# Graph attention on one core: score halves issued in the other order, and layer-norm normalizations moved from VectorE to ScalarE

## The chip, the cores and the metric

The kernel runs on one core of a Trainium2 chip. The metric is the time of one execution on the device, in microseconds (us); the median of several runs is compared. The profile comes from one further execution with the hardware profiler on.

The core's engines run side by side and each works through its own queue in program order: TensorE (PE in the rows, its weight loads PEld), VectorE (DVE), ScalarE (ACT), GpSimd (POOL), and SyncE (SP), which issues the DMAs. They wait for each other through semaphores. TensorE writes its results to PSUM, a small memory that VectorE and ScalarE read; GpSimd works on SBUF, the large on-chip memory, only.

## The reference

The input is `x` (8 frames, 2048 nodes, 256 channels, float32) and an adjacency matrix `adj` (2048 x 2048). With `LN(x) = (x - mean) * rsqrt(var + 1e-5)` over the channels:

```python
q, k, v = split(einsum('fnc,ck->fnk', x, w_qkv), 3)       # 8 heads of 32 channels
scores = einsum('fnhd,fmhd->fhnm', q, k) / sqrt(32)
attn   = softmax(where(adj > 0, scores, -1e9), axis=-1)
t      = einsum('fhnm,fmhd->fnhd', attn, v)
y      = LN(x + t) * ln1_g + ln1_b
h      = relu(y @ w1 + b1)
z      = LN(y + h @ w2 + b2) * ln2_g + ln2_b
out    = LN(x + z)
```

So each node passes three layer norms: after the attention, after the two-layer network, and after the outer residual.

## The kernel before

**The attention steps.** For each frame `f` the queries are cut in 4 chunks of 512 (`qc`), the 8 heads in 2 groups of 4 (`g`), the keys in 16 blocks of 128 (`mb`). One step handles one `(f, qc, g, mb)`; there are 8 x 4 x 2 x 16 = 1024 steps. In this text S(k) is the score part on TensorE of step k, A0(k) and A1(k) are its two additions on VectorE, E(k) its exponential on ScalarE, V(k) its value part on TensorE.

- `scores(item)` (L135 to L146). For each half (two heads) a PSUM tile `s` of 128 x 1024 takes the two heads' score matmuls, L142. Each head is a 32-row matmul in its own strip of 32 rows of the array and has two matmul instructions in the trace, so a step has 8. Then VectorE adds the mask out of PSUM into half of the tile `p` (L144: A0, then A1), and ScalarE takes the exponential of the whole tile `p` in place (L146: E).
- `values(item)` (L152 to L183). Four heads' value matmuls add into `o` (L161). In 9 of 16 blocks (`POOLED`, mb 0, 1, 3, 4, 6, 7, 9, 10, 12) GpSimd adds the tile `p` to `acc` (L165, L167: 8 additions to a group of 16 steps); in the others the row sums go through TensorE into `den` (L175). At the last block `acc` goes into `den` too, and ScalarE copies `o` and `den` out (L181, L183).
- The main loop emits S, A and E of step t+2, then V of step t, then one piece of filler work. The queues follow that order.
- `ps_s` has three PSUM tiles `s`, handed out in turn. Two of them go to each step, and one to every filler piece that needs PSUM. So between filler pieces the first half of step k reuses the tile that A1(k-2) freed, and the second half the tile that A0(k-1) freed. There are 5 tiles `p`; A(k) can be written once V and GpSimd are through with the tile of step k-5.

**The filler.** After 32 steps a chunk's `tail(f, qc)` (L204 to L275) is put in a queue and carried out a piece at a time, one piece per step, during the first half of the next chunk. It divides by the row sums, adds `x`, and does the three norms with the two-layer network between. A norm is `norm_stats` (L186: statistics on VectorE, L190 and L191, then `rs`, the inverse standard deviation, on GpSimd, L193 and L194), two pieces later `norm` (L197, L199: four VectorE instructions, one for each of 128 rows of the tile `y`), and then what follows:

- norm 1 (called at L232, filler piece of block 4): in the next piece TensorE transposes `y` (L237), ScalarE applies gain and bias (L240), GpSimd does the same on `y` itself (L242, L243); then L248 and L258 are the two-layer network and L260 its residual.
- norm 2 (L264, block 10): followed by three GpSimd operations on the same tile (L265 to L267).
- norm 3 (L274, block 15): followed by the store.

There are 32 tails, so 96 norms and 384 instructions at L199. In the last query chunk of a frame the projections of the next frame are filler too.

`general_path` runs only if a guard finds the row sums out of range.

Of the kernel before, what the change touches and what calls it, by code (L numbers as in the profile page):

```python
# [10 lines left out]
F32 = mybir.dt.float32  # L11
# [3 lines left out]
AF = mybir.ActivationFunctionType  # L15
ALU = mybir.AluOpType
AX = mybir.AxisListType

P = 128
H = 8  # L20
D = 32
CH = 512
# [30 lines left out]
def fast_path(ctx, tc, cst, x, adj, out, RS):  # L53
    nc = tc.nc
    F, N, C = x.shape
    NT, NCK, TPC, MB = N // P, N // CH, CH // P, N // P
# [10 lines left out]
    small = ctx.enter_context(tc.tile_pool(name="small", bufs=6))  # L67
    ps_s = ctx.enter_context(tc.tile_pool(name="ps_s", bufs=3, space=bass.MemoryType.PSUM))
# [32 lines left out]
    QT, KT, V = {}, {}, {}  # L101
# [33 lines left out]
    def scores(item):  # L135
        f, qc, g, mb = item
        pt = PT[item] = pp.tile([P, 4, CH], F32, name="p")
        for half in range(2):
            ps = ps_s.tile([P, 2, CH], F32, name="s")
            for j in range(2):  # L140
                r = D * (2 * half + j)
                nc.tensor.matmul(ps[:, j, :], KT[f, mb // TPC][r:r + D, g, (mb % TPC) * P:(mb % TPC + 1) * P],  # L142
                                 QT[f, qc][r:r + D, g, :], start=True, stop=True)
            nc.vector.tensor_tensor(pt[:, 2 * half:2 * half + 2, :], ps,  # L144
                                    mask[:, mb, qc * CH:(qc + 1) * CH][:, None, :].to_broadcast([P, 2, CH]), ALU.add)
        nc.scalar.activation(pt, pt, AF.Exp, scale=1.0 / math.sqrt(D))  # L146
# [48 lines left out]
        return mv, rs  # L195

    def norm(t, mv, rs):  # L197
        for j in range(TPC):
            nc.vector.tensor_scalar(t[:, j, :], t[:, j, :], mv[:, j, 0:1], rs[:, j:j + 1], op0=ALU.subtract, op1=ALU.mult)  # L199

    def rows(v):
        return v[:, None, :].to_broadcast([P, TPC, C])
# [1 line left out]
    def tail(f, qc):  # L204
# [25 lines left out]
        yield  # L230
        yield
        norm(y, mv, rs)  # L232
        yield
        py = ps_s.tile([P, 2, CH], F32, name="s")
# [27 lines left out]
        yield  # L262
        yield
        norm(z, mv, rs)  # L264
        nc.gpsimd.tensor_tensor(z, z, rows(cst["g2r"]), ALU.mult)  # L265
        nc.gpsimd.tensor_tensor(z, z, rows(cst["be2r"]), ALU.add)
# [5 lines left out]
        yield  # L272
        yield
        norm(z, mv, rs)  # L274
        nc.sync.dma_start(out[f, qc * CH:(qc + 1) * CH, :].rearrange("(j p) c -> p j c", p=P), z)  # L275

# [20 lines left out]
    for k in range(LEAD):  # L297
        scores(items[k])
    for t, item in enumerate(items):
        f, qc, g, mb = item  # L300
        if f == 0 and g == 0 and mb == 0 and qc + 1 < NCK:
            fill.append(mask_ahead(qc + 1))
        if f + 1 < F:
            if qc == NCK - 1 and g == 0 and mb == 0:
                fill.append(project(f + 1, 0))
                fill.append(project(f + 1, 1))
            if qc == NCK - 1 and g == 1 and mb == 9:
                fill.append(project(f + 1, 2))
                fill.append(project(f + 1, 3))
        if t + LEAD < len(items):  # L310
            nf, _, _, nmb = items[t + LEAD]
            while (nf, nmb // TPC) not in V:
                advance()
            scores(items[t + LEAD])
        values(item)
        if mb == MB - 1 and g == 1:
            fill.append(tail(f, qc))
        advance()
# [236 lines left out]
```

## Time and profile before

| what | value |
|---|---|
| median of 3 runs | 4457.56 us (4450.9 to 4458.03) |
| the profiled execution's own time | 4455.42 us |
| its span, first to last instruction | 4453.5 us |
| mean granted TensorE clock | 0.925 of full speed |
| busy: PE / DVE / ACT / POOL | 3876.9 / 3170.7 / 2259.6 / 2896.5 us |

How to read it: busy time is the union of an engine's instructions, as an average over stages with different limits. An instruction of VectorE or GpSimd that is held up after its start counts as busy for all that time. Windows of the trace are given in us from the start of the span. Where single stages are looked at, the chunk that starts at 908.8 us stands for the others.

### The profile page before, as it was taken

What the parts mean: (1) busy time and instruction counts of PE and PEld (TensorE: products, weight loads), DVE (VectorE), ACT (ScalarE), POOL (GpSimd) and SP (SyncE); (2) the same over time, 40 slices, a digit from 0 to 9 for tenths busy, and PEclk for the clock granted to TensorE, in tenths of its full rate; (3) what the DMA queues carried; (4) which work ended last, traced back from release to release, by engine and by line L of the source; (5) the groups of instructions that cost most, each with busy time, mean ns of one, the idle gap of its engine ahead of it and who ended that gap; (6) DMA issues with size and microseconds to landing.
All of it is one profiled execution on the core that took longest, in us unless ns stands there. A gap on an engine that the chain in (4) does not pass through costs nothing.

```text
span 4453.5 us, 56008 instructions
## 1 busy us (share of the span) xinstructions
PE 3876.9 (87%) x23556; PEld 1271.3 (29%) x23556; DVE 3170.7 (71%) x3463; ACT 2259.6 (51%) x1425; POOL 2896.5 (65%) x905
## 2 busy tenths in 40 slices
PE   7888898888988889888898888988889898888896
PEld 3222232222322223222232222322233222322222
DVE  2777757777478775778657876678856777577775
ACT  3644554555555545455455554455554455444553
POOL 1665647677467765678656776577765677567776
PEclk9988899999999999899999999999999899999998
DMA  3010000000000000000000000000000000000000
GB/s 108 10 48 29 20 29 10 10 10 1 29 10 10 10 29 1 10 10 10 29 1 10 10 10 29 1 10 10 10 29 1 10 11 10 29 10 6 6 10 15
DMA packets 62003, 72.72 MB, mean 16 GB/s; under 512 B 2993, under 2 KB 53297, under 8 KB 61745
## 3 DMA queue, kind: packets, MB, share of 16 engines
q1 hardware_dynamic: 61744, 69.09, 5.0%
q8 instruction: 186, 3.05, 0.3%
q14 instruction: 73, 0.59, 0.0%
HBM read 52.30 MB, written 16.78 MB: 16 GB/s over the span
## 4 chain that ended last, share of the span: by engine, by line
PE 35%; DVE 24%; issue 18%; POOL 17%; ACT 5%; DMA 1%; SPq 0%; POOLq 0%; ACTq 0%; DVEq 0%
DVE p L144 14%; POOL acc L167 13%; PE s L142 11%; PE o L161 8%; DVE y L199 7%; PE s L117 5%; ACT p L146 4%; PE s L248 3%; PE s L126 3%; POOL acc L165 2%; PE den L175 2%; POOL y L226 1%; PE s L237 1%; DVE st L190 1%; DMA in<-in_x_dram 1%
## 5 line engine op out<-in xcount | busy, mean ns | idle before, releaser
L144 DVE TENSOR_TENSOR p<-s,mask 128x1024 f32<-128x1024 f32 x2048 | 2378.7, 1216 | 977.0 <-PE s L142 939.1
L146 ACT ACTIVATE p<-p 128x2048 f32<-128x2048 f32 x1024 | 1958.0, 1912 | 1931.1 <-DVE p L144 1897.1
L167 POOL TENSOR_TENSOR acc<-acc,p 128x2048 f32<-128x2048 f32 x448 | 2039.3, 4552 | 420.6 <-ACT p L146 403.2
L142 PE MATMUL s<-qT,kT 32*128 32x512 f32 x8192 | 1592.0, 688 | 281.4 <-DVE p L144 276.4
L161 PE MATMUL o<-p,v 128*32 128x512 f32 x8192 | 1172.1, 646 | 38.8 <-ACT oT L181 36.8
L142 PEld LDWEIGHTS s<-qT,kT 32*128 32x128 f32 x8192 | 485.4, 195 | 1220.2 <-DVE p L144 689.8
L165 POOL TENSOR_TENSOR acc<-p 128x2048 f32<-128x2048 f32 x64 | 291.8, 4559 | 343.1 <-ACT p L146 343.1
L175 PE MATMUL den<-p,ones 128*32 128x512 f32 x3584 | 476.7, 604 | 0.0
L199 DVE TENSOR_SCALAR y<-y,mv,rs 128x256 f32<-128x256 f32 x384 | 471.1, 1287 | 4.3 <-POOL rs L194 4.3
L161 PEld LDWEIGHTS o<-p,v 128*32 128x32 f32 x8192 | 165.6, 111 | 905.7 <-issue 659.9
L226 POOL TENSOR_TENSOR y<-y,in 128x1024 f32<-128x1024 f32 x32 | 75.6, 2363 | 377.2 <-DVE y L223 377.2
L117 PE MATMUL s<-turned,wqkv 128*128 128x512 f32 x512 | 240.6, 615 | 11.3 <-ACT turned L111 11.3
L175 PEld LDWEIGHTS den<-p,ones 128*32 128x32 f32 x3584 | 118.5, 112 | 279.9 <-issue 279.9
L193 POOL TENSOR_SCALAR rs<-mv 128x4 f32<-128x4 f32 x96 | 18.5, 193 | 256.5 <-DVE mv L191 251.9
L237 PE MATMUL s<-ident,y 128*128 128x128 f32 x256 | 71.8, 411 | 126.6 <-DVE y L199 126.6
L190 DVE BATCH_NORM_STATS2 st<-y 128x6 f32<-128x256 f32 x384 | 154.0, 401 | 10.3 <-POOL y L267 7.8
L117 PEld LDWEIGHTS s<-turned,wqkv 128*128 128x128 f32 x512 | 94.2, 193 | 159.0 <-issue 128.0
L248 PE MATMUL s<-turned,w1s 128*128 128x512 f32 x256 | 133.2, 668 | 0.9 <-ACT turned L240 0.9
L242 POOL TENSOR_TENSOR y<-y,g1r 128x1024 f32<-128x1024 f32 x32 | 75.3, 2353 | 71.4 <-PE s L237 69.4
L258 PE MATMUL s<-w2s,hT 128*128 128x256 f32 x512 | 119.2, 386 | 0.8 <-ACT hT L251 0.8
L126 PE MATMUL s<-wqkv,turned 128*128 128x256 f32 x512 | 118.6, 385 | 0.0
L260 DVE TENSOR_TENSOR y<-s,y 128x1024 f32<-128x1024 f32 x32 | 39.2, 1224 | 109.9 <-issue 97.3
(53 smaller groups left out, 1516.7 us busy)
## 6 DMA issues: line engine op xcount, KB each, us to landing
in<-in_x_dram SPq DMA_DIRECT2D x64, 512.0 KB, 5.8
in<-in_adj_dram SPq DMA_DIRECT2D x32, 512.0 KB, 4.7
out_dram<-y SPq DMA_DIRECT2D x32, 512.0 KB, 3.2
wqkv<-in_L_gnn_w_qkv_dram SPq DMA_DIRECT2D x1, 768.0 KB, 4.6
w1s<-in_L_gnn_w_dram SPq DMA_DIRECT2D x1, 256.0 KB, 4.9
w2s<-in_L_gnn_w_dram SPq DMA_DIRECT2D x1, 256.0 KB, 5.2
g1r<-in_L_gnn_ln_g_dram SPq DMA_DIRECT2D x1, 128.0 KB, 4.4
g2r<-in_L_gnn_ln_g_dram SPq DMA_DIRECT2D x1, 128.0 KB, 6.3
```

The source lines that it names most:

```text
L117: nc.tensor.matmul(ps[:, g, :], wqkv[:, a, k0 + g * P:k0 + (g + 1) * P], xT[:, a, :], start=(a == 0), stop=(a == 1))
L126: nc.tensor.matmul(psv[:, j, :], xT[:, a, j * P:(j + 1) * P], wqkv[:, a, 2 * C:], start=(a == 0), stop=(a == 1))
L142: nc.tensor.matmul(ps[:, j, :], KT[f, mb // TPC][r:r + D, g, (mb % TPC) * P:(mb % TPC + 1) * P], QT[f, qc][r:r + D, g, :], start=True, sto ...
L144: nc.vector.tensor_tensor(pt[:, 2 * half:2 * half + 2, :], ps, mask[:, mb, qc * CH:(qc + 1) * CH][:, None, :].to_broadcast([P, 2, CH]), AL ...
L146: nc.scalar.activation(pt, pt, AF.Exp, scale=1.0 / math.sqrt(D))
L161: nc.tensor.matmul(O[grp][r:r + D, :], V[f, mb // TPC][:, mb % TPC, g * P + r:g * P + r + D], pt[:, h, :], start=(mb == 0), stop=(mb == LAST))
L165: nc.gpsimd.tensor_tensor(ACC[grp], PT[f, qc, g, POOLED[0]], pt, ALU.add)
L167: nc.gpsimd.tensor_tensor(ACC[grp], ACC[grp], pt, ALU.add)
L175: nc.tensor.matmul(DEN[grp][r:r + D, :], cst["ones"], term[:, h, :], start=(mb == first), stop=(n == 1))
L190: nc.vector.bn_stats(st, t[:, j, :])
L199: nc.vector.tensor_scalar(t[:, j, :], t[:, j, :], mv[:, j, 0:1], rs[:, j:j + 1], op0=ALU.subtract, op1=ALU.mult)
L248: nc.tensor.matmul(ph[:, d, :], w1s[:, a, d * P:(d + 1) * P], yT[:, a, :], start=(a == 0), stop=(a == 1))
```

## The change

In `scores` both PSUM tiles are taken first; the matmuls of the second half are emitted ahead of those of the first half, and the two mask additions come after all of them, in the old order. In `norm` the four VectorE instructions `(t - mean) * rs` become one small VectorE instruction that makes `nb = -mean * rs` (128 x 4) and four ScalarE activations `Identity(t * rs + nb)` with scale and bias per row. `norm` serves all three norms of a tail.

```diff
@@ scores
         pt = PT[item] = pp.tile([P, 4, CH], F32, name="p")
-        for half in range(2):
-            ps = ps_s.tile([P, 2, CH], F32, name="s")
+        ps2 = [ps_s.tile([P, 2, CH], F32, name="s") for _ in range(2)]
+
+        for half in (1, 0):
             for j in range(2):
                 r = D * (2 * half + j)
-                nc.tensor.matmul(ps[:, j, :], KT[f, mb // TPC][r:r + D, g, (mb % TPC) * P:(mb % TPC + 1) * P],
+                nc.tensor.matmul(ps2[half][:, j, :], KT[f, mb // TPC][r:r + D, g, (mb % TPC) * P:(mb % TPC + 1) * P],
                                  QT[f, qc][r:r + D, g, :], start=True, stop=True)
+        for half, ps in enumerate(ps2):
             nc.vector.tensor_tensor(pt[:, 2 * half:2 * half + 2, :], ps,
                                     mask[:, mb, qc * CH:(qc + 1) * CH][:, None, :].to_broadcast([P, 2, CH]), ALU.add)
         nc.scalar.activation(pt, pt, AF.Exp, scale=1.0 / math.sqrt(D))
@@ norm
     def norm(t, mv, rs):
+        nb = small.tile([P, TPC], F32, name="nb")
+        nc.vector.scalar_tensor_tensor(nb, mv[:, :, 0], -1.0, rs, op0=ALU.mult, op1=ALU.mult)
         for j in range(TPC):
-            nc.vector.tensor_scalar(t[:, j, :], t[:, j, :], mv[:, j, 0:1], rs[:, j:j + 1], op0=ALU.subtract, op1=ALU.mult)
+            nc.scalar.activation(t[:, j, :], t[:, j, :], AF.Identity, bias=nb[:, j:j + 1], scale=rs[:, j:j + 1])
```

## Rows read from the trace of the kernel before

**Rows 1.** The page: busy time of each engine, and the chain that ended last.

```profile
PE 3876.9 (87%) x23556; PEld 1271.3 (29%) x23556; DVE 3170.7 (71%) x3463; ACT 2259.6 (51%) x1425; POOL 2896.5 (65%) x905
...
DVE p L144 14%; POOL acc L167 13%; PE s L142 11%; PE o L161 8%; DVE y L199 7%; PE s L117 5%; ACT p L146 4%; PE s L248 3%; PE s L126 3%; POOL acc L165 2%; PE den L175 2%; POOL y L226 1%; PE s L237 1%; DVE st L190 1%; DMA in<-in_x_dram 1%
```

**Rows 2.** Groups by line: busy us, mean ns | idle before, releasers.

```profile
L144 DVE TENSOR_TENSOR p<-s,mask 128x1024 f32<-128x1024 f32 x2048 | 2378.7, 1216 | 977.0 <-PE s L142 939.1 <-POOL acc L167 28.1 <-POOL acc L165 8.3
L167 POOL TENSOR_TENSOR acc<-acc,p 128x2048 f32<-128x2048 f32 x448 | 2039.3, 4552 | 420.6 <-ACT p L146 403.2
...
L142 PE MATMUL s<-qT,kT 32*128 32x512 f32 x8192 | 1592.0, 688 | 281.4 <-DVE p L144 276.4 <-ACT mask L97 4.8
...
L199 DVE TENSOR_SCALAR y<-y,mv,rs 128x256 f32<-128x256 f32 x384 | 471.1, 1287 | 4.3 <-POOL rs L194 4.3
...
L191 DVE BATCH_NORM_AGGREGATE mv<-st 128x2 f32<-128x6 f32 x384 | 69.9, 182 | 13.0
...
L240 ACT ACTIVATE turned<-s,be1c,g1c 128x512 f32<-128x512 f32 x64 | 45.7, 765 | 12.6 <-PE s L237 12.6
...
L181 ACT COPY oT<-o 128x512 f32<-128x512 f32 x64 | 36.3, 567 | 1.2 <-PE o L161 1.2
...
L111 ACT COPY turned<-s 128x1024 f32<-128x1024 f32 x32 | 32.2, 1008 | 36.3 <-PE s L110 36.3
```

**Rows 3.** Line L199 alone: duration ns, minimum/median/maximum.

```profile
L199 DVE TENSOR_SCALAR y<-y,mv,rs x384: 399/405/4681, 218.5 to 4448.1; 128x256 f32<-128x256 f32 x192
```

**Rows 4.** Groups by line, VectorE, 938 to 941 us: the second L199 of one norm 1.

```profile
L199 DVE TENSOR_SCALAR y<-y,mv,rs 128x256 f32<-128x256 f32 x1 | 4.7, 4656 | 0.0
```

**Rows 5.** Groups by line, VectorE, 969.6 to 970.9 us: the first L199 of norm 2.

```profile
L199 DVE TENSOR_SCALAR y<-y,mv,rs 128x256 f32<-128x256 f32 x1 | 1.7, 1651 | 0.0
```

**Rows 6.** Timeline around norm 1: start us, us, engine, line, tiles, [idle before <-releaser].

```profile
935.70 6.72 DVE L199 TENSOR_SCALAR y<-y,mv,rs 128x256 f32<-128x256 f32 x4
...
935.88 1.91 ACT L146 ACTIVATE p<-p 128x2048 f32<-128x2048 f32 x1 [0.35 <-DVE p L144]
...
941.83 1.98 PE L237 MATMUL s<-ident,y 128*128 128x128 f32 x7 [3.89 <-DVE y L199]
...
943.74 3.08 PE L142 MATMUL s<-qT,kT 32*128 32x512 f32 x8
```

**Rows 7.** Windows of one tail: us, busy us (count) of PE, PEld, DVE, ACT, POOL, granted clock.

```profile
941.80:948.60 6.80, 6.77 (x23) 2.50 (x23) 5.24 (x6) 3.46 (x4) 4.63 (x2) 0.50 0.01 2
...
975.90:982.80 6.90, 5.33 (x20) 1.22 (x20) 4.92 (x6) 3.80 (x2) 6.28 (x3) 0.51 0.00 0
```

**Rows 8.** Timeline of GpSimd alone through the same tail.

```profile
924.23 2.36 POOL L226 TENSOR_TENSOR y<-y,in 128x1024 f32<-128x1024 f32 x1 [13.09 <-DVE y L223]
...
943.89 2.35 POOL L242 TENSOR_TENSOR y<-y,g1r 128x1024 f32<-128x1024 f32 x1 [2.27 <-PE s L237]
...
965.07 0.19 POOL L193 TENSOR_SCALAR rs<-mv 128x4 f32<-128x4 f32 x1 [7.23 <-DVE mv L191]
...
976.36 2.36 POOL L265 TENSOR_TENSOR y<-y,g2r 128x1024 f32<-128x1024 f32 x1 [0.88 <-DVE y L199]
...
988.49 1.02 POOL L194 TENSOR_TENSOR rs<-rs,mhalf 128x4 f32<-128x4 f32 x1
```

**Rows 9.** Timeline of three steps without filler.

```profile
2083.29 1.14 PE L142 MATMUL s<-qT,kT 32*128 32x512 f32 x8
...
2084.54 6.93 DVE L144 TENSOR_TENSOR p<-s,mask 128x1024 f32<-128x1024 f32 x6 [0.82 <-PE s L142]
...
2085.36 1.59 PE L142 MATMUL s<-qT,kT 32*128 32x512 f32 x8
2085.82 0.30 PEld L142 LDWEIGHTS s<-qT,kT 32*128 32x128 f32 x4 [0.16 <-DVE p L144]
...
2090.99 1.14 PE L142 MATMUL s<-qT,kT 32*128 32x512 f32 x8
```

**Rows 10.** The waits, longest in total: us in all, times, longest.

```profile
PEld s L142 <- DVE p L144: 689.8, 668, 7.2
```

## The prediction

> **What bounds the kernel now.** I read the page first, then the groups by line, the waits, and last the timelines of single chunks. On the page no engine is full [rows 1]: TensorE is busy for 3876.9 us of 4453.5, VectorE for 3170.7, GpSimd for 2896.5, ScalarE for 2259.6. The chain is spread over three engines too: L144 on VectorE 14%, L167 on GpSimd 13%, L142 on TensorE 11%, L199 on VectorE 7%. An average like that hides two kinds of stretch, which the timelines tell apart.
>
> Without filler, TensorE works without a pause. Three steps (two in GpSimd's list, one with row sums on TensorE) take 2090.99 - 2083.29 = 7.70 us [rows 9].
>
> With a tail in the filler it is another picture. The first norm of the tail holds VectorE for 6.72 us, from 935.70, and TensorE stands for 3.89 us before the transposes that need its result [rows 6]. Then its clock is at 0.50, the lower of its two levels (1.2 GHz), for 6.8 us; after norm 2 it is at 0.51 for 6.9 us [rows 7]. At that level one step's score matmuls take 3.08 us [rows 6], against 1.14 at the full clock [rows 9].
>
> Why is the norm so long? An instruction of L199 takes 0.399 us at least, 0.405 in the median and 4.681 at most, where the mean is 1.287 [rows 2, 3]. So 384 x 0.405 = 156 us would do, and 471 - 156 = 315 us are waiting inside the instruction. The long ones last as long as one GpSimd addition of 4.552 us [rows 2]: in the norm shown the second instruction took 4.656 [rows 4]. The two engines evidently shut each other out while GpSimd works, and VectorE gets in between two of its additions.
>
> **Part 1, the norms: what goes and what comes.**
>
> Taken off VectorE: 96 x 4 instructions, 471 us, 4.9 us a norm.
>
> Added on VectorE: 96 instructions that make `nb`, on 4 elements a row. The trace has none like it; the nearest small one is L191 with 0.182 us [rows 2]. Its floor is about that. It reads two operands from SBUF, so it may be shut out as L199 is; its ceiling is then 4.7 us [rows 3], one GpSimd addition. Between the ends I take the wait of a norm's first instruction, since `nb` stands in the same place in VectorE's queue and GpSimd is usually in the middle of an addition: 1.65 us in norm 2 [rows 5]. The second instruction's full wait then has no successor, as there is no second instruction.
>
> The Trainium skill ("SBUF — State Buffer", section "Who interferes with whom") states that a VectorE instruction with two SBUF inputs contends with a GpSimd instruction that reads SBUF, and that the other side is blocked for the whole instruction. For L199 the trace agrees with the blocking (4.656 us [rows 4]); for an instruction like `nb` no row of before shows it. By that rule the removed contention comes back once a norm instead of up to twice, which is the value taken; without it each norm would be some 1.4 us shorter still on VectorE.
>
> Added on ScalarE: 384 activations on 128 x 256. L240 is the nearest, with scale and bias from tiles: 0.765 us for 512 elements a row [rows 2]. From L181 and L111, 512 elements cost 1.008 - 0.567 = 0.441 us, so 256 fewer save 0.22: 0.54 us each, about 1.9 us a norm with a slight overlap, 96 x 1.9 = 182 us in all. The floor is 0.35 us each (L181 less 0.22), 1.4 a norm; the ceiling 0.765, some 3.0 a norm. ScalarE goes from 51% to 55%. What hides it: the four stand behind E of the step that is emitted with them, and what queues behind them is the next E, whose additions on VectorE need about 2.3 us (6.93 / 6 x 2 [rows 9]) anyway. If that cover were gone, it would cost 1.9 us a norm.
>
> What that does in the tail shown. *Norm 1:* the first L199 ended at about 937.0 (935.70 + 6.72, less 4.66 and two of 0.4 [rows 3, 4, 6]), and `nb` would too. E ends at 935.88 + 1.91 = 937.8 [rows 6], the four activations at 939.7, and the transposes, which follow them one by one, at 940.3. Before they ended at 941.83 + 1.98 = 943.8: 3.5 us won. If the clock stays up, scores and values behind them need 2.2 us instead of 4.9, another 2 us or so once the wait for L240 is allowed for: 5.5 in all. *Norm 2:* `nb` holds VectorE for 1.65 instead of 6.87 us, another 5 us, and the slow window behind it [rows 7] gets shorter.
>
> **Where the gain meets GpSimd.** This would be over 12 us a tail, but GpSimd's work in it stays: from the start of L226 at 924.23 to the end of L194 at 988.49 + 1.02 = 989.5 are 65.3 us [rows 8]. Eight additions, six operations of the tail (2.36 each) and three pairs for `rs` (1.2 each) make 8 x 4.55 + 6 x 2.36 + 3 x 1.2 = 54. So its idle time, some 10.9 us (2.27 before L242, 7.23 before L193, 0.88 before L265 and small ones [rows 8]), is the most that a tail can win before GpSimd is full. By my count the first gap closes, the second goes from 7.2 to about 4 (the residual sum comes 5.5 us earlier, GpSimd is through only 2.3 us earlier), the third closes. After norm 2 TensorE would be 12 us ahead and must wait for L267, whose output norm 3's statistics need, and they hold VectorE's queue. GpSimd's chain so wins 6.5 us, and VectorE, which now turns to norm 3 as soon as `rs` is there, about 8. I take 7 us. 31 tails x 7 = 217 us. The last tail has no other work beside it; there each norm is longer by about 0.7 us (ScalarE's 1.9 and a small instruction against 4 x 0.4), 2 us in all.
>
> **Part 2, the order of the halves.** No instruction is added. The four heads' matmuls run side by side: all 8 instructions take 1.14 us when they start together [rows 9]. When they are apart, the first pair starts at once (2085.36) and the second when A0 of the step before frees its tile (2085.82); the end is 2085.36 + 1.59 = 2086.95, 1.13 us after that release [rows 9]. So the 1.59 is no longer work than 1.14, it is an earlier start. In the new order the pair that must wait comes first and the free one is behind it. TensorE ends at the same time, but A0, which needs the half that was free, can start only then. Before, A0 followed A1 without a gap (six additions in 6.93 us [rows 9]); now it starts some 0.1 us behind the end of all four pairs. Worked through the three steps: S to S is 1.13 for the matmuls, 0.11 to VectorE, 1.155 for A0, 0.12 back to TensorE = 2.52 us, twice, and about 3.0 in the step with row sums, where TensorE sets the pace: 8.05 instead of 7.70, +0.35.
>
> Floor of the cost: nothing, where TensorE is late and all tiles are free. Ceiling: 668 times a weight load of L142 waits for VectorE [rows 10]; each at 0.25 us makes 167. Between: 25 half chunks carry neither tail nor projection, with four such triples each, 25 x 4 x 0.35 = 35 us. In these GpSimd is at its limit as well (two additions, 9.1 us, in 7.70) and now makes VectorE wait for 28.1 us in all [rows 2]; that wait shrinks as the steps get longer. The splits inside the tails lie behind GpSimd's chain. So 35 us, nearer the floor.
>
> **Sum.** 4455.4 - 217 + 2 + 35 = 4275 us; the profiled execution is 2 us below the median of the runs, too little to change the number.
>
> **The rivals.**
>
> *Slower: the order of the halves decides.* Every split step loses its head start and VectorE's gap is not absorbed: +167 us. With tails that shrink by half of my estimate, 3.5 us, the time is 4455 + 167 - 31 x 3.5 = 4513. For it: the 668 waits [rows 10]. Against it: L167 and L199 hold 20% of the chain [rows 1], and in a stretch that GpSimd sets a later A0 costs nothing. Point of decision: a tail that shrinks by under 167 / 31 = 5.4 us.
>
> *The matmuls together are cheaper.* If the 1592 us of L142 [rows 2] were work, 1024 joint steps x 1.14 = 1167 would save up to 425 us; with half of that on the path and the norms' gain the time would be 4455 - 217 - 213 = 4025. The Trainium skill ("TensorEngine Tiling (Array Packing)", "Key Properties") says that different tiles can execute in parallel, which speaks for it; the trace agrees that they do, but already in the old order (1.14 us for all). Against it: the end 1.13 us after the release [rows 9].
>
> *Norms closer to the ceiling of GpSimd's idle time.* 31 x 10.9 = 338, less the 35 of part 2: about 4150.
>
> *ScalarE's four come late.* With `nb` blocked for a full addition and ScalarE behind it, the transposes start as late as before and the clock falls as before. Norm 1 wins nothing, norm 2 some 3 us: 31 x 3 - 35 = 58 won, 4400.
>
> **How the numbers follow.** The forecast's neighbourhood (4200 to 4360) has 0.50; the two rivals with a larger gain 0.20 together; the late norms (4360 to 4445) 0.13; the rest, 0.17, is the slower rival and what lies around zero. A change below 0.2% (9 us) is about what a measurement of this kernel can't tell from none. Faster 0.82, same 0.04, slower 0.14. The range leaves out the slower rival and the far end of the large gains: 4160 to 4435.
>
> **What the profile after should show.** L199 as 384 ScalarE activations of about 0.5 us; `nb` with a median well under 0.3 us but some up to 4.6; VectorE's busy time lower by about 380 us; the mean clock above 0.925; TensorE's wait at L237 half as long; GpSimd's gap before L193 smaller; L142's busy time near 1200 us, with VectorE's waits for it longer; three steps without filler at 8.0 us. The prediction is wrong if tails do not shrink though L199 is gone (then ScalarE or GpSimd carried them), or if the stretches without filler grow by more than 5%.

## The result and the profile after

| | before | after |
|---|---|---|
| median | 4456.33 us (4450.9 to 4458.03, 4 runs) | 4292.55 us (4284.15 to 4297.27, 4 runs) |
| span of the profiled execution | 4453.5 us | 4288.7 us |
| mean granted TensorE clock | 0.925 | 0.937 |

The ratio is 0.9632, with a 95% interval of 0.9614 to 0.965: 164 us faster. The forecast was 4275.

The page after, busy time of each engine and the chain by line, beside [rows 1]:

```profile
PE 3825.8 (89%) x23556; PEld 1252.1 (29%) x23556; DVE 2825.3 (66%) x3175; ACT 2443.5 (57%) x1809; POOL 2897.6 (68%) x905
...
POOL acc L169 17%; PE s L143 12%; PE o L163 7%; DVE p L146 7%; PE s L117 6%; ACT p L148 4%; PE den L177 3%; PE s L252 3%; PE s L126 3%; PE s L262 3%; POOL acc L167 2%; DVE st L192 2%; ACT y L203 2%; POOL y L270 2%; POOL y L271 2%
```

VectorE has 345 us less to do, ScalarE 184 us more. In the chain the mask additions fell from 14% to 7%, and the norms' 7% on VectorE became 2% on ScalarE; GpSimd's additions rose from 13% to 17%. GpSimd's work is the same as before; it now makes up more of that chain.

Groups by line after (columns as in [rows 2]):

```profile
L146 DVE TENSOR_TENSOR p<-s,mask 128x1024 f32<-128x1024 f32 x2048 | 2409.3, 1218 | 1054.8 <-PE s L143 994.8 <-ACT y L203 22.4 <-ACT dT L185 20.8
...
L143 PE MATMUL s<-qT,kT 32*128 32x512 f32 x8192 | 1554.6, 675 | 238.9 <-DVE p L146 233.8 <-ACT mask L97 5.1
...
L203 ACT ACTIVATE y<-y,nb,rs 128x256 f32<-128x256 f32 x384 | 198.4, 589 | 37.6 <-DVE nb L201 37.6
...
L241 PE MATMUL s<-ident,y 128*128 128x128 f32 x256 | 55.0, 303 | 36.6 <-ACT y L203 36.3
```

and line L201, which makes `nb`, alone, durations in ns, minimum/median/maximum:

```profile
L201 DVE SCALAR_TENSOR_TENSOR nb<-mv,rs x96: 150/1172/3471, 217.3 to 4281.3; 128x4 f32<-128x4 f32 x96
```

The four ScalarE activations take 0.589 us each. The new VectorE instruction works on four elements a row; it takes 0.150 us when nothing is in its way and 1.172 in the median. It is shut out by GpSimd, as the prediction assumed: 61 of the 96 take over 0.3 us, and each of these ends within 0.03 us behind the end of a long GpSimd operation; the other 35 take 0.150 to 0.163 us. The Trainium skill ("SBUF — State Buffer", "Who interferes with whom") states that a VectorE instruction with two SBUF inputs contends with a GpSimd instruction that reads SBUF; these ends, and the 1.172 beside the 0.150, agree.

The timeline around norm 1 of the same chunk, which now starts at 887.25 us (beside [rows 6]):

```profile
914.28 1.15 DVE L201 SCALAR_TENSOR_TENSOR nb<-mv,rs 128x4 f32<-128x4 f32 x1
914.40 1.91 ACT L148 ACTIVATE p<-p 128x2048 f32<-128x2048 f32 x1 [0.46 <-DVE p L146]
...
916.22 2.06 ACT L203 ACTIVATE y<-y,nb,rs 128x256 f32<-128x256 f32 x4
...
918.33 0.76 PE L241 MATMUL s<-ident,y 128*128 128x128 f32 x5 [0.16 <-ACT y L203]
919.02 1.14 PE L143 MATMUL s<-qT,kT 32*128 32x512 f32 x8
```

VectorE is held for 1.15 us instead of 6.72. The activations follow E directly, the transposes end at 919.1, and the next score matmuls take 1.14 us instead of 3.08: the granted clock is 1.00 from 919.02 to 921.40, where it was 0.50 before [rows 7].

GpSimd alone through this tail (beside [rows 8]):

```profile
902.60 2.37 POOL L230 TENSOR_TENSOR y<-y,in 128x1024 f32<-128x1024 f32 x1 [13.31 <-DVE y L227]
...
909.88 1.02 POOL L196 TENSOR_TENSOR rs<-rs,mhalf 128x4 f32<-128x4 f32 x1
...
919.99 2.38 POOL L246 TENSOR_TENSOR y<-y,g1r 128x1024 f32<-128x1024 f32 x1
...
937.99 0.19 POOL L195 TENSOR_SCALAR rs<-mv 128x4 f32<-128x4 f32 x1 [4.04 <-DVE mv L193]
938.27 1.02 POOL L196 TENSOR_TENSOR rs<-rs,mhalf 128x4 f32<-128x4 f32 x1
...
948.42 2.39 POOL L269 TENSOR_TENSOR y<-y,g2r 128x1024 f32<-128x1024 f32 x1
...
960.51 1.02 POOL L196 TENSOR_TENSOR rs<-rs,mhalf 128x4 f32<-128x4 f32 x1
```

From the first row to the end of the last are 58.9 us, before 65.3: 6.4 won. The gap before norm 1's gain operation is gone (2.27 before), the one before norm 2's statistics is 4.04 instead of 7.23, the one before L269 is gone (0.88 before). Behind norm 2 VectorE has a new wait, for GpSimd's last operation on the tile:

```profile
955.72 0.43 DVE L192 BATCH_NORM_STATS2 st<-y 128x6 f32<-128x256 f32 x1 [3.93 <-POOL y L271]
```

Three steps without filler (timeline, beside [rows 9]):

```profile
973.02 1.14 PE L143 MATMUL s<-qT,kT 32*128 32x512 f32 x8
...
974.30 2.36 DVE L146 TENSOR_TENSOR p<-s,mask 128x1024 f32<-128x1024 f32 x2 [0.59 <-PE s L143]
...
975.09 1.62 PE L143 MATMUL s<-qT,kT 32*128 32x512 f32 x8
975.58 0.30 PEld L143 LDWEIGHTS s<-qT,kT 32*128 32x128 f32 x4 [0.19 <-DVE p L146]
...
976.82 2.35 DVE L146 TENSOR_TENSOR p<-s,mask 128x1024 f32<-128x1024 f32 x2 [0.17 <-PE s L143]
...
981.01 1.14 PE L143 MATMUL s<-qT,kT 32*128 32x512 f32 x8
```

They take 7.99 us instead of 7.70. VectorE now pauses 0.17 us ahead of the second pair of additions, where six followed each other without a gap before.

### The profile page after: what moved, and what is told of

Same layout as the page of the kernel before. It is cut to its first block, busy times and chain, and to the rows that moved or that the text cites. A ratio compares the mean times of both kernels' runs of the same rounds, so it can differ in the third digit from the quotient of the medians.

```text
span 4288.7 us, 56201 instructions
## 1 busy us (share of the span) xinstructions
PE 3825.8 (89%) x23556; PEld 1252.1 (29%) x23556; DVE 2825.3 (66%) x3175; ACT 2443.5 (57%) x1809; POOL 2897.6 (68%) x905
## 4 chain that ended last, share of the span: by engine, by line
PE 37%; POOL 26%; issue 15%; DVE 12%; ACT 7%; DMA 1%; SPq 0%; DVEq 0%; POOLq 0%; ACTq 0%
POOL acc L169 17%; PE s L143 12%; PE o L163 7%; DVE p L146 7%; PE s L117 6%; ACT p L148 4%; PE den L177 3%; PE s L252 3%; PE s L126 3%; PE s L262 3%; POOL acc L167 2%; DVE st L192 2%; ACT y L203 2%; POOL y L270 2%; POOL y L271 2%
## 5 line engine op out<-in xcount | busy, mean ns | idle before, releaser
L146 DVE TENSOR_TENSOR p<-s,mask 128x1024 f32<-128x1024 f32 x2048 | 2409.3, 1218 | 1054.8 <-PE s L143 994.8
L143 PE MATMUL s<-qT,kT 32*128 32x512 f32 x8192 | 1554.6, 675 | 238.9 <-DVE p L146 233.8
L163 PE MATMUL o<-p,v 128*32 128x512 f32 x8192 | 1158.7, 639 | 18.5 <-ACT oT L183 17.3
L143 PEld LDWEIGHTS s<-qT,kT 32*128 32x128 f32 x8192 | 476.1, 192 | 1166.0 <-DVE p L146 623.5
L167 POOL TENSOR_TENSOR acc<-p 128x2048 f32<-128x2048 f32 x64 | 291.9, 4562 | 329.7 <-ACT p L148 287.1
L177 PE MATMUL den<-p,ones 128*32 128x512 f32 x3584 | 495.2, 626 | 0.0
L192 DVE BATCH_NORM_STATS2 st<-y 128x6 f32<-128x256 f32 x384 | 154.3, 402 | 103.4 <-POOL y L271 101.0
L203 ACT ACTIVATE y<-y,nb,rs 128x256 f32<-128x256 f32 x384 | 198.4, 589 | 37.6 <-DVE nb L201 37.6
L252 PE MATMUL s<-turned,w1s 128*128 128x512 f32 x256 | 121.7, 619 | 11.2 <-ACT turned L244 11.2
L269 POOL TENSOR_TENSOR y<-y,g2r 128x1024 f32<-128x1024 f32 x32 | 76.2, 2380 | 54.7 <-ACT y L203 54.7
L262 PEld LDWEIGHTS s<-w2s,hT 128*128 128x128 f32 x512 | 94.6, 190 | 39.4 <-DVE p L146 20.1
```

The source lines that it names most:

```text
L143: nc.tensor.matmul(ps2[half][:, j, :], KT[f, mb // TPC][r:r + D, g, (mb % TPC) * P:(mb % TPC + 1) * P], QT[f, qc][r:r + D, g, :], start=Tr ...
L163: nc.tensor.matmul(O[grp][r:r + D, :], V[f, mb // TPC][:, mb % TPC, g * P + r:g * P + r + D], pt[:, h, :], start=(mb == 0), stop=(mb == LAST))
L167: nc.gpsimd.tensor_tensor(ACC[grp], PT[f, qc, g, POOLED[0]], pt, ALU.add)
L177: nc.tensor.matmul(DEN[grp][r:r + D, :], cst["ones"], term[:, h, :], start=(mb == first), stop=(n == 1))
L203: nc.scalar.activation(t[:, j, :], t[:, j, :], AF.Identity, bias=nb[:, j:j + 1], scale=rs[:, j:j + 1])
L252: nc.tensor.matmul(ph[:, d, :], w1s[:, a, d * P:(d + 1) * P], yT[:, a, :], start=(a == 0), stop=(a == 1))
```

## The experiments

All ratios are to the kernel before, in runs on the same chip; between the chips its median ran from 4452 to 4458, so a difference in us between two experiments is uncertain by some 5 us. Line numbers shift with each edit. Where the text names no other kernel, the edit is to the changed one.

**1 and 2: each part alone.** The first has the new `norm` and the old `scores`; the second the other way round.

> The norms on ScalarE as changed, the score halves in the old order. The prediction's theory (the new order costs a little, some 35 us): 4250 to 4265, ratio near 0.955, and three steps without filler at 7.70 us again. Rival 1 (the order of the halves costs as much as every lost head start, up to 167 us): 4130 to 4200. Rival 2 (the order is where part of the gain comes from, the four heads' matmuls together being less work): above 4300.

> The score halves in the new order, the norms on VectorE as before. Theory: slower by 20 to 60 us, 4475 to 4515, ratio 1.005 to 1.015; steps without filler 7.70 -> 8.0 us for three; the tails as long as before, since VectorE's blocked norms set them. Rival 1: slower by 100 to 167 us. Rival 2: faster than before.

Measured: norms alone 4256.83 us, ratio 0.9554 (0.9538 to 0.957); order alone 4510.42, ratio 1.0126 (1.0109 to 1.0143), beside 4454.31. The norms give 197 us, and the order takes 36 on top of them (4292.55 - 4256.83) and 56 without them. So the split depends on which part is put first: with the order first the norms give 218 (4510.42 - 4292.55). Why the order costs 20 us more without the norms was not separated. The profiles show that its mean clock was then 0.915 against 0.925 before, and 0.937 with and without the order once the norms were moved. Rival 2 of the first, that the order is part of the gain, falls; so does rival 1, that every lost head start counts (up to 167). Without the new order, three steps without filler take 983.22 - 975.52 = 7.70 us again (timeline of the kernel with the norms alone):

```profile
975.52 1.14 PE L142 MATMUL s<-qT,kT 32*128 32x512 f32 x8
...
983.22 1.14 PE L142 MATMUL s<-qT,kT 32*128 32x512 f32 x8
```

**3 and 4: is GpSimd's chain the limit, after and before?** One of GpSimd's operations of each tail is taken out, of the kernel after and of the one before.

```diff
         nc.gpsimd.tensor_tensor(z, z, rows(cst["g2r"]), ALU.mult)
-        nc.gpsimd.tensor_tensor(z, z, rows(cst["be2r"]), ALU.add)
         nc.gpsimd.tensor_tensor(z, z, xs, ALU.add)
```

> The changed kernel without one GpSimd operation of each tail: the addition of the second norm's bias is left out (2.36 us, 76 us in all). Theory: in the changed kernel GpSimd's chain sets the tail from norm 2 to norm 3, so nearly all of it comes back: 4292 - 60 to 75 = 4217 to 4232. Rival (ScalarE or TensorE sets it): 4275 to 4292.

> The kernel before without the same GpSimd operation (the second norm's bias is left out). Theory: there VectorE's blocked norm 2 sets the tail, and the statistics of norm 3 come 2 us after GpSimd is through, so little comes back: 0 to 25 us, 4432 to 4457. Rival (GpSimd was the limit before as well): 60 to 75 us less, 4382 to 4397.

Measured: after, 4172.45 us, ratio 0.937 (0.9355 to 0.9386), 120 us less than the changed kernel; before, 4441.62, ratio 0.9973 (0.9962 to 0.9984), 13 us less. So what GpSimd does behind norm 2 was hardly the limit before and is now. But 120 us came back for 76 us of work, 45 below the range expected. What VectorE's statistics wait for GpSimd fell only from 101.0 us to 36.0 in all (the waits, kernel after and kernel 3):

```profile
DVE st L192 <- POOL y L271: 101.0, 29, 9.5
```

```profile
DVE st L192 <- POOL y L270: 36.0, 19, 7.0
```

Where the rest comes from is not separated. The clock's mean rose from 0.937 to 0.956 beside it (cores view of kernel 3):

```profile
core 0: 4169.1 us, clock 0.956
```

With only two levels, full and half, that is (1 - 0.937) x 2 x 4289 = 540 us at the lower one against 367. In the changed kernel the stretch behind this wait is one at half clock, with TensorE busy for 4.49 of 6.80 us (windows, kernel after, columns as in [rows 7]); that a shorter wait saves part of that as well is argued, not shown.

```profile
956.80:963.60 6.80, 4.49 (x16) 1.10 (x20) 5.61 (x10) 1.91 (x1) 4.56 (x3) 0.50 0.00 0
```

**5 and 6: norm 1 alone and norm 2 alone on ScalarE,** the other two as before, both with the new order. `norm_v` is the old `norm`; below is the first of the two.

```diff
-        norm(z, mv, rs)
+        norm_v(z, mv, rs)
...
-        norm(z, mv, rs)
+        norm_v(z, mv, rs)
```

> The changed kernel with norm 1 alone on ScalarE; norms 2 and 3 on VectorE again. All three together are worth 218 us against the new order alone (4510 to 4292). Theory (a common limit, GpSimd's chain, caps what they give together): norm 1 alone 3.5 to 5.5 us a tail, 4340 to 4400, and its gain plus norm 2's alone is more than 218. Rival (each norm's gain stands by itself): the two gains add up to 218 or less.

> The changed kernel with norm 2 alone on ScalarE; norms 1 and 3 on VectorE. Theory: 2 to 5 us a tail, 4355 to 4450, since GpSimd's chain behind norm 2 allows no more; more than 218 together with norm 1's own gain. Rival as for norm 1 alone.

Measured: norm 1 alone 4315.29 us, 0.9689 (0.9673 to 0.9706); norm 2 alone 4494.97, 1.0092 (1.0075 to 1.0109). Against the order alone (4510.42) norm 1 gives 195 us and norm 2 gives 15; the two together 210 of 218. The theory in these expectations, that each alone would give more than its share, falls: norm 1 is nearly all of it, and norm 2 gave little even where norm 1 was still blocked. Norm 3 was not run alone; some 7 us are left for it and for what the norms do together. For norm 2, GpSimd's timeline says why. These are the two ends of its stretch from norm 2's `rs` to norm 3's in kernel 5:

```profile
956.76 1.02 POOL L196 TENSOR_TENSOR rs<-rs,mhalf 128x4 f32<-128x4 f32 x1
967.77 2.35 POOL L273 TENSOR_TENSOR y<-y,g2r 128x1024 f32<-128x1024 f32 x1 [0.88 <-DVE y L207]
...
979.91 1.02 POOL L196 TENSOR_TENSOR rs<-rs,mhalf 128x4 f32<-128x4 f32 x1
```

With norm 2 on VectorE they are 23.15 us apart, as before the change (965.34, shown further down, to 988.49 in [rows 8]); with it on ScalarE 960.51 - 938.27 = 22.24. GpSimd was working through that stretch with 0.88 us of idle time, so no more than 0.9 us was to be had there, however long VectorE was held. Over all 32 tails this idle time is 55.8 us in kernel 5, 1.7 a tail. In the changed kernel it is still 54.7 us, but in 8 tails.

**7 and 8: `nb` on GpSimd, and a longer norm on ScalarE.**

```diff
-        nc.vector.scalar_tensor_tensor(nb, mv[:, :, 0], -1.0, rs, op0=ALU.mult, op1=ALU.mult)
+        nc.gpsimd.tensor_scalar(nb, mv[:, :, 0], 0.0, -1.0, op0=ALU.add, op1=ALU.mult)
+        nc.gpsimd.tensor_tensor(nb, nb, rs, ALU.mult)
```

> The changed kernel with the small tile nb made on GpSimd behind rs (two small operations) instead of on VectorE. If nb's mean of 0.94 us on VectorE (0.15 at least) is waiting for GpSimd, VectorE loses 90 us of busy time and no wait of that kind is left; GpSimd, which is the limit, has 0.3 to 1 us more a norm. Theory: little, 4265 to 4320. Rival (what VectorE waits for in nb sets the tail): 4200 to 4240.

Measured: 4451.43 us, 0.9995 (0.9984 to 1.0006). The whole gain is lost, which neither theory had. The expectation called the place "behind rs"; as built, `nb` stands in `norm`, two filler pieces later, behind two additions of GpSimd. Operations of 0.19 and 0.20 us so waited behind two additions of some 9.2 us together, and ScalarE with them (the waits):

```profile
ACT y L204 <- POOL nb L202: 251.6, 58, 11.5
```

> The changed kernel with each of the four ScalarE activations of a norm cut into two of 128 columns: the same elements, eight instructions instead of four, some 1 to 1.5 us more ScalarE time a norm (about 100 to 140 us in all). Theory (ScalarE is covered in norms 2 and 3, and only norm 1's transposes wait for it): 4292 + 10 to 45 = 4302 to 4337. Rival (ScalarE's norms lie on the path everywhere): 4390 or more.

```diff
-        for j in range(TPC):
-            nc.scalar.activation(t[:, j, :], t[:, j, :], AF.Identity, bias=nb[:, j:j + 1], scale=rs[:, j:j + 1])
+        for j in range(2 * TPC):
+            half = slice((j % 2) * P, (j % 2 + 1) * P)
+            nc.scalar.activation(t[:, j // 2, half], t[:, j // 2, half], AF.Identity, bias=nb[:, j // 2:j // 2 + 1],
+                                 scale=rs[:, j // 2:j // 2 + 1])
```

Measured: 4368.04 us, 0.98 (0.9783 to 0.9816), 75 us more than the changed kernel for 107 us more ScalarE time (groups by line):

```profile
L204 ACT ACTIVATE y<-y,nb,rs 128x128 f32<-128x128 f32 x768 | 305.9, 483 | 32.3 <-DVE nb L201 32.3
```

That lies between the two expectations; ScalarE's time is not as well covered as the prediction had it. In the chunk shown, GpSimd's stretch from the first `rs` to the second grew by 2.0 us, from 938.27 - 909.88 = 28.39 to 960.02 - 929.63 = 30.39, and the next from `rs` to `rs` stayed at 22.2 (982.25 - 960.02). So in this chunk the cost is in norm 1, where 1.1 us more on ScalarE make 2 us:

```profile
929.63 1.02 POOL L196 TENSOR_TENSOR rs<-rs,mhalf 128x4 f32<-128x4 f32 x1
...
960.02 1.02 POOL L196 TENSOR_TENSOR rs<-rs,mhalf 128x4 f32<-128x4 f32 x1
...
982.25 1.02 POOL L196 TENSOR_TENSOR rs<-rs,mhalf 128x4 f32<-128x4 f32 x1
```

The timeline shows where they come from. TensorE stands 1.8 us in four pieces among the transposes of this norm, where the row of the changed kernel has 0.16. In the 3.7 us behind them its granted clock is 0.54, against 1.00 in the 2.4 us behind those of the changed kernel.

**9: the bias addition moved.** Norms on ScalarE, old order of the halves; the bias of norm 2 goes into `xs` while GpSimd waits for norm 2's statistics.

```diff
+        nc.gpsimd.tensor_tensor(xs, xs, rows(cst["be2r"]), ALU.add)
         z = y
         nc.vector.tensor_tensor(z, pfv, y, ALU.add)
         mv, rs = norm_stats(z)
...
         nc.gpsimd.tensor_tensor(z, z, rows(cst["g2r"]), ALU.mult)
-        nc.gpsimd.tensor_tensor(z, z, rows(cst["be2r"]), ALU.add)
         nc.gpsimd.tensor_tensor(z, z, xs, ALU.add)
```

> Norms on ScalarE, old order of the halves (4257), and the second norm's bias added to the residual x ahead of norm 2's statistics, where GpSimd waits, instead of behind norm 2: the same operations, one of them earlier. Theory (GpSimd's chain from norm 2 to norm 3 sets the tail; without that operation 120 us were won): 4135 to 4170. Rival (only less work on GpSimd helps, its place doesn't matter): 4240 to 4260.

Measured: 4144.38 us, 0.9309 (0.9293 to 0.9324), 112 us less than the norms alone with the same operations. So the place of this addition in GpSimd's queue counts, and not only the amount of work.

**10 to 12: three steps on from there.** `nb` on GpSimd again, now in `norm_stats` right behind `rs`; block 12 of the group beside the tail summed on TensorE; and the first of these with norm 1 emitted one piece earlier.

```diff
+        nb = small.tile([P, TPC], F32, name="nb")
+        nc.gpsimd.tensor_scalar(nb, mv[:, :, 0], 0.0, -1.0, op0=ALU.add, op1=ALU.mult)
+        nc.gpsimd.tensor_tensor(nb, nb, rs, ALU.mult)
-        return mv, rs
+        return nb, rs
...
```

> The kernel with the moved bias addition (4144), with nb made on GpSimd right behind rs, in the statistics piece, ahead of the next additions in its queue. When it stood two pieces later, behind two additions, the change cost 159 us. Theory (the place in GpSimd's queue cost that, not the operation): 4110 to 4165, and VectorE has no nb and no wait for GpSimd of that kind. Rival (small operations on GpSimd are dear in themselves): 4250 or more.

Measured: 4170.75 us, 0.9359 (0.9344 to 0.9375), 26 us more than kernel 9, a little above what the theory had, but far from kernel 7, which cost 159 us (4451.43 - 4292.55). The same two operations are cheap in this place and dear in that one. The kernels around them differ as well, in the order of the halves and the moved addition, so the two prices are not an exact pair.

```diff
+        pooled = POOLED if g else POOLED[:-1]
...
-        elif mb in POOLED[2:]:
+        elif mb in pooled[2:]:
...
-        terms = [] if mb in POOLED else [pt]
+        terms = [] if mb in pooled else [pt]
```

> The kernel with the moved bias addition (4144), with block 12 of the group that runs beside the tail summed on TensorE instead of GpSimd: 4.56 us less GpSimd work a tail, 1.04 us more TensorE work (33 us in all). Theory (GpSimd's chain still sets the tail behind norm 2): 4050 to 4110. Rival (TensorE sets it by now): 4165 to 4180.

Measured: 4144.15 us, 0.9291 (0.9276 to 0.9307), no change against kernel 9 that is clear of noise (the intervals of the ratios overlap). 146 us of GpSimd's work (32 x 4.56) were exchanged for 33 on TensorE for nothing. The theory falls for this kernel, in which GpSimd's chain does not set the tail by itself; the rival, 4165 or more, missed too. A gain on GpSimd may have been used up by the 33 us, and the additions on GpSimd (L167 there, L168 here) are 21% of the chain in both kernels, so what holds kernel 9 is open.

```diff
         mv, rs = norm_stats(y)
         yield
-        yield
         norm(y, mv, rs)
         yield
+        yield
```

> The kernel with the moved bias addition and nb made on GpSimd right behind rs (4171), with norm 1 emitted one filler piece earlier and its transposes where they were. Cutting ScalarE's activations in two made norms 1.1 us longer and cost 75 us, all of it ahead of norm 2's statistics. Theory (TensorE waits for norm 1 on ScalarE, and then runs at the lower clock): with the norm out of the way by then, 4090 to 4140, and no wait of L237's successor for ScalarE. Rival (TensorE's wait is hidden by GpSimd's chain): 4160 to 4180.

Measured: 4145.09 us, 0.9299 (0.9283 to 0.9314), 26 us less than kernel 10 and 5 above the range expected. TensorE's wait for norm 1 is gone but for one tail (the waits, kernel 10 and kernel 12), and the mean clock is 0.958 instead of 0.949:

```profile
PE s L240 <- ACT y L202: 40.5, 110, 9.4
```

```profile
PE s L240 <- ACT y L202: 9.4, 1, 9.4
```

So the fastest kernels run are 9, 11 and 12, at 4144 to 4145 us, 3.5% below the changed kernel and 7% below the one before.

## Why the prediction came out as it did

**The sum** was 217 - 2 for the norms and 35 for the order; measured, 197 and 36. In that split the 17 us by which the forecast was too low are in the term for the norms, 7 us a tail where the runs give 197 / 32 = 6.2. In the other split, the order first, the norms' 218 meet the forecast and the order's 56 is the term that was too small. The runs don't decide between the two; the prediction reckoned the order on top of the shortened tails, which is the first.

**The blocked norm, right.** The normalizations on VectorE were mostly waiting for GpSimd, and one small instruction in their place still waits: 90 us of busy time for 96 of them (0.94 each, where 1.65 was taken). Only its median was foretold wrongly: "well under 0.3 us" against 1.172.

**Norm 1, right in place and size.** 5.5 us a tail were predicted. GpSimd's stretch from the first `rs` to the second shrank by 5.5, from 33.85 us before to 28.39 after, and the run with norm 1 alone gave 195 / 32 = 6.1. The two ends before:

```profile
931.49 1.02 POOL L194 TENSOR_TENSOR rs<-rs,mhalf 128x4 f32<-128x4 f32 x1
...
965.34 1.02 POOL L194 TENSOR_TENSOR rs<-rs,mhalf 128x4 f32<-128x4 f32 x1
```

TensorE's wait for these transposes (L237, now L241) fell from 126.6 us in all to 36.3, more than the half that was named.

**Norm 2, right only through its cap.** "Another 5 us" on VectorE is what the instruction got shorter, and was rightly not added up: GpSimd's idle time ahead of L265 was 0.88 us in the chunk shown, and the run gave 15 / 32 = 0.5. The prediction named the wait for GpSimd's last operation on the tile (L267, now L271). It still let VectorE win 8 us by turning to norm 3 earlier, and took 7 instead of GpSimd's 6.5; that wait came to 101.0 us in all. In the first split this is the term that was mis-sized: with 6.5 it would have been 31 x 6.5 - 2 = 200 us, against 197 measured.

**GpSimd as the new limit, right:** 6.5 us were predicted for its chain in a tail, 6.4 measured in the chunk shown; that it limits the tail behind norm 2 is shown by runs 3 and 9, with run 4 for the contrast. Once this wait is eased, less work on GpSimd brought nothing (run 11), and norm 1 out of TensorE's way 26 us (run 12). What holds the tail then was not separated.

**ScalarE's cover, wrong in part.** "What hides it" holds for norm 2 in the chunk shown (the stretch behind it did not move in run 8); for norm 3 no run shows it. In norm 1 the transposes wait for ScalarE, and 1.1 us more there cost 2. The prediction did count those transposes as waiting; it did not say that the time is then uncovered.

**The order, right in size in part by luck, wrong in mechanism.** The step said that "the pair that must wait comes first and the free one is behind it", with both starting together. The trace after shows the first pair starting early as before (975.09) and the second waiting for A0 of the step before (975.58). From these starts I infer, since the trace does not number the tiles, that the PSUM tile freed longest ago still goes to the pair emitted first. But that is now the second half, and A0 needs the first, which is the late one. So A0 starts behind the end of the late pair, as predicted, by another way: 7.99 us for three steps against 8.05. By the prediction's own count the 0.29 make 25 x 4 x 0.29 = 29 us of the 36, and the 56 without the norms it does not explain. The early start also makes L143's busy time 1554.6 us, not the "near 1200" that I named. The rival that the matmuls together are cheaper was therefore not tested by any run, as the pairs still start apart. What speaks against it is that here too all four are through 1.13 us after the release (975.09 + 1.62 - 975.58). The same order with the additions swapped too, so that A0 meets the early pair, was not tried.

## What to carry to other kernels

When an instruction's mean is three times its median, look for the engine that shuts it out, and price its removal by the stretch behind it: here one of three identical norms gave 195 of the 218 us and another 15, and behind that one GpSimd had next to no idle time to give. Ask which engine's queue is next to be full, and where in it the operations stand. Two small operations behind a backlog cost 159 us, and a 2.4 us one, in each of 32 tails, moved into a gap gave 112. Of a step's halves that take turns in three buffers, the one consumed first should be the one whose buffer is free first; the other way round cost 36 to 56 us here.

## What the runs showed of the hardware beyond that

Time came back that was more than the work taken out: 76 us less on GpSimd returned 120 us, with the mean clock up from 0.937 to 0.956. In kernel 8, 1.1 us more of ScalarE in norm 1 let TensorE stand 1.8 us between the transposes; then its granted clock was 0.54 for 3.7 us, near the lower of its two levels, and the tail grew by 2 us. A VectorE instruction on 4 elements a row took up to 3.47 us while GpSimd was adding, against 0.150 undisturbed, and each of the 61 long ones ended right behind a GpSimd operation.
